# Row broadcasts for a state scan: one 128-partition transfer with a repeated source pattern in place of four 32-partition transfers

## The chip, the cores and the metric

The kernel runs on one core of one Trainium2 chip, as one program in one launch. The metric is device time in microseconds (us) of one execution. Three executions before the change took 7948.8, 7950.06 and 7962.73 us; the median is 7950.06 us.

## The reference

The input `x` is 4 x 512 x 64 x 64 in float32, that is 4 batches of 512 channels and 4096 positions. Two layers follow each other, each with a residual: `x = x + L0(groupnorm(x))`, then `x = x + L1(groupnorm(x))`. L0 is a state-space layer; L1 is a linear attention with 8 heads. The change lies in L0, whose core is this:

```python
xn = layer_norm(xf, norm_g, norm_b)                 # 512 channels, cut into 4 chunks of 128
xz = einsum('bld,ed->ble', chunk, in_proj_w); xi, z = split(xz, 2)      # 256 inner channels
xc = silu(causal_conv4(xi) + conv_b)
dbc = einsum('bld,ed->ble', xc, x_proj_w)
dt, Bs, Cs = dbc[..., :8], dbc[..., 8:24], dbc[..., 24:]
dt = softplus(einsum('blr,er->ble', dt, dt_proj_w) + dt_proj_b)
def step(h, inp):                                    # scan over 4096 positions
    dt_t, B_t, C_t, x_t = inp
    h = exp(dt_t[:, :, None] * A) * h + (dt_t * x_t)[:, :, None] * B_t[:, None, :]
    return h, einsum('bds,bs->bd', h, C_t)           # 16 states for each of 256 channels
y = (ys + xc * D_param) * silu(z)
ym = einsum('bld,od->blo', y, out_proj_w) + skip_scale * chunk
```

The row `B_t` of a state is the same for all channels, and so is the row `C_t`. On the chip each such row has to stand on every partition that holds a channel of that state.

## The kernel before

**Tiling.** The work is cut into steps `(b, t, c)`: 4 batches, 8 tiles of 512 positions (`T`), 4 chunks of 128 channels, so 128 steps. A step has 16 slots (`SLOTS`), 2,048 in all. The 256 inner channels of a step are two halves `e` of 128. Within a half the 16 states are taken in `NQ` = 4 groups `q` of `KS` = 4 states. One tile holds 4 states x 32 channels (`BLK` = 32) on its 128 partitions: partitions 0 to 31 are the first state of the group, 32 to 63 the second, and so on. The four blocks of 32 channels, index `j`, lie side by side in the free dimension. A pair of slots (`jj` = 0, 1) handles one group `q` of one half.

**What a pair of slots does.**
- `b_row(g)` (line 692) brings the four B rows of a group to the 128 partitions of a tile `b_all`, 128 x 512 float32. There are three such buffers. It is called in the first slot of a pair, for the group three pairs on.
- `c_tail(g)` (line 697) does the same with the last quarter (128 positions) of the four C rows, into `c_sb`, 128 x 128 float32, two buffers. It is called in the second slot of a pair, for the next pair.
- Both call `for_states(dst, rows_, q)` (line 685), the function that is changed. `rows_` is a tile in DRAM, 16 rows of 512 (or of 128) positions, stored once per step at lines 659 and 660.
- `drive` (line 717, GpSimd) multiplies `d_all` by `b_all` into `bx`; it runs two slots ahead. `decay` (line 708, ScalarE) makes `dA` = exp(A dt); the scan at line 739 (VectorE) makes `h` from both.
- The product of `h` with the C row is cut in two. VectorE does 384 of the 512 positions (line 759), with a C row that TensorE brought into PSUM (`c_row`). GpSimd does the last 128 (line 751), with `c_sb`. TensorE then sums the states into `y`.

**Other transfers of the loop.** `spread` (line 633, transfers at line 639) is called twice in a step. It fills `d_all`, 128 partitions x 16 KB, from two DRAM tiles, with eight transfers of 256 KB, each to 32 partitions. Loads and stores of whole 1 MB tiles (`xn`, `xs`, `x`, `xa`, `xb`) and stores of results go by the same queue.

**What sets the order.** The order of instructions on each engine is written out by hand: `slot` calls the functions above, and `after` the work of neighbouring steps. All these transfers are issued by SyncE (SP) in program order. SP waits at a transfer for the buffer that it overwrites, and for the semaphore that it signals: there are eight of them, used in turn, and each transfer waits until the one eight before it has landed. Only the adding load `xr` is issued by GpSimd, and weight loads ahead of the loop by ScalarE.

Of the kernel before, what the change touches and what calls it, by code (L numbers as in the profile page):

```python
# [24 lines left out]
def kernel(  # L25
# [24 lines left out]
    nc = tc.nc  # L50
# [8 lines left out]
    BLK = 32  # L59
    KS = P // BLK  # L60
# [623 lines left out]

    def for_states(dst, rows_, q):

        for k in range(KS):
            nc.sync.dma_start(  # L688
                dst[k * BLK : (k + 1) * BLK, :], rows_[q * KS + k, :].partition_broadcast(BLK)
            )  # L690

    def b_row(g):
        n, e, q, _ = place(g)
        b_all[g // JJ] = wk.tile([P, T], F32, tag="b_all", name=f"b_all_{g}", bufs=3)
        for_states(b_all[g // JJ], fs[n]["b_rows"], q)

    def c_tail(g):
        n, e, q, _ = place(g)
        c_sb[g // JJ] = wk.tile([P, T - CUT], F32, tag="c_sb", name=f"c_sb_{g}", bufs=2)
        for_states(c_sb[g // JJ], fs[n]["c_rows"], q)  # L700
# [539 lines left out]
```

## Time and profile before

| What | Value |
|---|---|
| median of three executions | 7950.06 us |
| the profiled execution's own time | 7963.09 us |
| its span on the core | 7961.4 us |
| mean granted TensorE clock | 0.897 |
| busy VectorE (DVE), GpSimd (POOL) | 6977.7 us (88%), 6880.5 us (86%) |
| busy TensorE (PE), ScalarE (ACT) | 6453.6 us (81%), 5507.6 us (69%) |
| transfers to `b_all` | 4,096 of 64.0 KB |
| transfers to `c_sb` | 4,096 of 16.0 KB |
| transfers to `d_all` | 2,048 of 256.0 KB |

The profile is of one execution. A busy time counts the time in which an engine runs an instruction; the issuing of transfers by SP is not in it and is shown as `SPq`. DMA packets are the pieces that the 16 DMA engines of the core move one by one: a row of a transfer is one packet, and each engine that takes part in a transfer writes one more, of 4 bytes, to the semaphore at its end. "Share of 16 engines" is the summed time of packets over 16 times the length of the stretch; packets of one engine can overlap a little, so that it can pass 100%. The first 100 us are preparation and the first step's inputs, and the last 480 us are the rest of the attention of the last batch; the 2,048 slots lie between.

### The profile page before, as it was taken

To read this page: it belongs to the slowest core of one execution; us is meant where nothing else is said; L and a number is where in the kernel's file an instruction comes from. 1 tells how busy PE (TensorE), PEld (TensorE's weight loads), DVE (VectorE), ACT (ScalarE), POOL (GpSimd) and SP (SyncE) were. 2 spreads that over 40 slices of the span, in tenths; PEclk is the share of its full clock that TensorE was granted. 3 is DMA by queue.
4 is the path that set the end of the run, shared out by engine and by line. 5 is a ranking of instruction groups with operands and counts; after the bars stand their busy time and mean duration, and the time that the engine had idled before them with its cause. 6 is when DMAs were issued, how large, how long until landed. Compare 5 with 4: busy or idle time off the path is not lost.

```text
span 7961.4 us, 90563 instructions
## 1 busy us (share of the span) xinstructions
PE 6453.6 (81%) x24835; PEld 2120.0 (27%) x24880; DVE 6977.7 (88%) x5766; ACT 5507.6 (69%) x8321; POOL 6880.5 (86%) x4597
## 2 busy tenths in 40 slices
PE   5676777677789888888788888898688888888599
PEld 1121212112223222322222223332122332322144
DVE  5999999999999999989999999998999999988600
ACT  4667777777777777767777777677777777777421
POOL 4999999999999899989999899898999999889600
PEclk7888888888899999998899999899899999999799
DMA  5666666666666666777766666677666666676402
GB/s 154 167 168 166 151 155 159 160 155 167 169 179 162 151 163 159 174 189 175 174 155 171 171 157 161 155 185 189 156 167 163 161 161 159 145 194 180 112 32 90
DMA packets 829184, 1265.87 MB, mean 159 GB/s; under 512 B 183912, under 2 KB 317560, under 8 KB 816384
## 3 DMA queue, kind: packets, MB, share of 16 engines
q1 hardware_dynamic: 804736, 1222.32, 61.1%
q0 software_dynamic: 16896, 33.56, 2.4%
q10 hardware_dynamic: 7040, 4.20, 0.2%
q8 instruction: 195, 3.19, 0.2%
q14 instruction: 317, 2.60, 0.1%
HBM read 1052.78 MB, written 206.57 MB: 158 GB/s over the span
## 4 chain that ended last, share of the span: by engine, by line
DVE 33%; PE 21%; ACT 15%; DMA 12%; issue 8%; SPq 6%; POOL 6%; POOLq 0%; ACTq 0%; DVEq 0%
DVE h L739 22%; DVE h L759 9%; DMA d_all<-d_rows 7%; ACT dA L713 5%; PE pq L124 5%; POOL bx L721 4%; PE pc L124 4%; SPq L688 3%; PE y L124 3%; PE pr L124 3%; SPq L639 2%; DMA c_sb<-c_rows 2%; ACT xz L1048 2%; PE po L124 2%; ACT L1048 1%
## 5 line engine op out<-in xcount | busy, mean ns | idle before, releaser
L721 POOL TENSOR_TENSOR bx<-d_all,b_all 128x1024 f32<-128x1024 f32 x2048 | 4824.7, 2367 | 213.3 <-DVE h L739 195.1
L739 DVE TENSOR_TENSOR_SCAN h<-dA,st,bx 128x512 f32<-128x512 f32 x3584 | 4358.9, 1264 | 358.7 <-ACT dA L713 159.0
L713 ACT ACTIVATE dA<-d_all,a_t 128x512 f32<-128x512 f32 x4096 | 2752.9, 687 | 1568.5 <-DVE h L739 1521.8
L759 DVE TENSOR_TENSOR h<-h,c_all 128x1536 f32<-128x1536 f32 x1024 | 1767.5, 1726 | 0.1
L751 POOL TENSOR_TENSOR h<-h,c_sb 128x512 f32<-128x512 f32 x1024 | 1300.2, 1270 | 190.2 <-DMA c_sb<-c_rows 95.2
L124 PE MATMUL y<-h,fold 128*32 128x512 f32 x8192 | 1271.2, 696 | 71.6 <-POOL h L751 67.4
L124 PE MATMUL c_all<-parts,sel 128*128 128x384 bf16 x1024 | 369.9, 361 | 1123.3 <-DVE h L759 1121.7
L124 PE MATMUL pc<-xn,w_cv 128*128 128x512 f32 x2048 | 1045.7, 645 | 122.8 <-DVE xn L414 62.1
L124 PE MATMUL pq<-w_qk,xa 128*128 128x512 f32 x2048 | 965.5, 604 | 7.9 <-issue 5.3
L739 DVE TENSOR_TENSOR_SCAN h<-dA,bx 128x512 f32<-128x512 f32 x512 | 591.2, 1203 | 90.0 <-ACT dA L713 65.1
L124 PEld LDWEIGHTS <-sel 128*128 128x128 bf16 x1280 | 127.1, 99 | 1762.2 <-DVE h L759 1562.5
L124 PEld LDWEIGHTS pc<-xn,w_cv 128*128 128x128 f32 x2048 | 389.5, 201 | 747.1 <-issue 424.7
L124 PEld LDWEIGHTS pq<-w_qk,xa 128*128 128x128 f32 x2048 | 398.6, 196 | 439.6 <-issue 422.4
L124 PE MATMUL pr<-xb,m 128*128 128x512 f32 x1024 | 485.3, 612 | 7.5 <-DMA xb<-x 3.6
L124 PE MATMUL pp<-xn,w_pr 128*128 128x512 f32 x1024 | 477.7, 597 | 4.8 <-DVE xn L414 4.8
L124 PEld LDWEIGHTS y<-h,fold 128*32 128x32 f32 x8192 | 170.6, 114 | 644.0 <-issue 344.9
L124 PE MATMUL y<-xz,dg 32*32 32x512 f32 x2048 | 337.3, 734 | 0.0
L781 POOL TENSOR_TENSOR xz<-xz 128x512 f32<-128x512 f32 x256 | 325.7, 1272 | 9.2 <-ACT xz L778 9.2
L832 ACT ACTIVATE kq<-pq 128x512 f32<-128x512 f32 x256 | 150.5, 588 | 259.9 <-PE pq L124 259.2
L124 PE MATMUL pd<-xz,w_xp 128*128 128x512 f32 x512 | 323.4, 764 | 7.8 <-ACT xz L1048 7.8
L628 POOL TENSOR_TENSOR dt<-dt,xz 128x1024 f32<-128x1024 f32 x128 | 302.3, 2361 | 24.7 <-ACT dt L620 24.6
L124 PE MATMUL pz<-xn,w_z 128*128 128x512 f32 x512 | 275.4, 631 | 11.7 <-ACT xz L608 8.2
(179 smaller groups left out, 6034.1 us busy)
## 6 DMA issues: line engine op xcount, KB each, us to landing
d_all<-d_rows SPq DMA_DIRECT2D x2048, 256.0 KB, 6.7
b_all<-b_rows SPq DMA_DIRECT2D x4096, 64.0 KB, 2.2
d_rows<-dt SPq DMA_DIRECT2D x256, 512.0 KB, 3.6
c_sb<-c_rows SPq DMA_DIRECT2D x4096, 16.0 KB, 1.8
xs<-in_x_dram SPq DMA_DIRECT2D x32, 1024.0 KB, 6.3
xn<-in_x_dram SPq DMA_DIRECT2D x32, 1024.0 KB, 6.2
xr<-in_x_dram POOLq DMA_DIRECT2D x32, 1024.0 KB, 10.7
x<-xr SPq DMA_DIRECT2D x32, 1024.0 KB, 4.2
```

The source lines that it names most:

```text
L124: nc.tensor.matmul(out_, lhsT, rhs, **how)
L628: nc.gpsimd.tensor_tensor(f["both"][:, 1], f["both"][:, 0], f["xz"][:, 0], ALU.mult)
L639: nc.sync.dma_start(d[k * BLK : (k + 1) * BLK, v], src)
L688: nc.sync.dma_start(dst[k * BLK : (k + 1) * BLK, :], rows_[q * KS + k, :].partition_broadcast(BLK))
L713: nc.scalar.activation(dAs[k], fs[n]["d_all", e][:, 0, j, :], AF.Exp, scale=a_t[:, e, j, q : q + 1])
L721: nc.gpsimd.tensor_tensor(bxs[g], fs[n]["d_all", e][:, 1, jj * 2 : jj * 2 + 2, :], bc(b_all[g // JJ], 2), ALU.mult)
L739: nc.vector.tensor_tensor_scan(h[:, j, :], dAs.pop(2 * g + i), bxs[g][:, i, :], 0.0 if t == 0 else st[:, c, e, q, j : j + 1], ALU.mult, AL ...
L751: nc.gpsimd.tensor_tensor(h[:, :, CUT:], h[:, :, CUT:], bc(c_sb.pop(g // JJ), NJ), ALU.mult)
L759: nc.vector.tensor_tensor(own, own, bc(c_all.pop(g // JJ), NJ), ALU.mult)
L781: nc.gpsimd.tensor_tensor(f["xz"][:, 1, e, :], f["xz"][:, 1, e, :], f["xz"][:, 0, e, :], ALU.mult)
L832: nc.scalar.activation(qk[i], pq, AF.Relu)
L1048: nc.scalar.activation(fs[n]["xz"], fs[n]["xz"], AF.Silu)
```

## The change

`for_states` issues one transfer for all 128 partitions. Its source is the four rows of the group with a middle dimension of step 0 that repeats each row 32 times: 4 x 32 x 512 (or 128) elements. Its destination is the whole tile, 128 partitions x 512 (or 128). Bytes and rows are the same as those of the four transfers together: 128 rows of 2 KB, or of 512 bytes. Nothing else in the kernel changes.

```diff
     def for_states(dst, rows_, q):
 
-        for k in range(KS):
-            nc.sync.dma_start(
-                dst[k * BLK : (k + 1) * BLK, :], rows_[q * KS + k, :].partition_broadcast(BLK)
-            )
+        src = rows_[q * KS : (q + 1) * KS, :].unsqueeze(1).to_broadcast([KS, BLK, dst.shape[-1]])
+        nc.sync.dma_start(dst, src)
```

In the built program SP then has 1,024 transfers to `b_all` and 1,024 to `c_sb` in place of 4,096 each, in the same places of its order.

## The prediction

> **What bounds the kernel now.** I first read busy time by stage, since start and end have other limits than the loop.
>
> ```profile
> core 0: us, PE busy (x) PEld busy (x) DVE busy (x) ACT busy (x) POOL busy (x), PEclk, DMA share, GB/s
> 0.00:100.00 100.00, 43.65 (x103) 20.42 (x104) 39.28 (x92) 23.14 (x31) 2.89 (x13) 0.81 0.44 139
> 100.00:7480.00 7380.00, 5976.39 (x23219) 1902.78 (x23246) 6900.82 (x5591) 5376.73 (x8118) 6863.62 (x4573) 0.90 0.67 166
> 7480.00:7961.00 481.00, 433.59 (x1518) 196.81 (x1530) 37.56 (x83) 107.73 (x173) 13.96 (x13) 0.94 0.18 62
> ```
>
> In the loop, 7380 us for 128 steps or 57.66 us a step, VectorE is busy 93.5% and GpSimd 93.0%. These two bound it. The DMA engines have work 67% of the time: no bound, but no small reserve either. Next, who waits for the tiles that change, from the waits on GpSimd:
>
> ```profile
> POOL bx L721 <- DVE h L739: 195.1, 290, 6.6
> POOL h L751 <- DMA c_sb<-c_rows: 95.2, 63, 6.6
> ...
> POOL bx L721 <- DMA d_all<-d_rows: 16.4, 1, 16.4
> ```
>
> So late transfers cost GpSimd little: 95.2 us for `c_sb` and 16.4 us for `d_all`; the answer for `b_all` adds 12.9 us of waits on ScalarE. A faster broadcast has some 124 us to win, 1.6%, unless it frees something that these waits don't show. Then the DMA queues and, for the loop alone, their load:
>
> ```profile
> q10 hardware_dynamic: 7040, 4.20, 0.2%
> ```
>
> ```profile
> q1 hardware_dynamic: 790226, 1184.28, 64.4%
> q0 software_dynamic: 16368, 32.51, 2.5%
> q8 instruction: 182, 2.98, 0.2%
> q14 instruction: 311, 2.55, 0.1%
> ```
>
> The second fence is the loop's: 67.2% of 57.66 us is 38.7 us of packet time a step on each of the 16 engines.
>
> **What the change removes.** Of 8,192 issues on SP, 6,144 go. Line 688 has a median of 419 ns each in the line's answer, so a tile's four cost 1.68 us. The new pattern has three dimensions on the source. The nearest row for a form of issue that isn't this one is `a_t` at line 295, with 586 to 747 ns and a median of 595 ns; one new issue should cost 0.42 to 0.75 us, and I take 0.595. SP saves 4.0 us per pair of slots less 1.2 (two tiles), some 2.2 us of 3.4. This lies off the path: SP is ahead of GpSimd wherever its waits are for buffers (`SPq L688 <- POOL st`, 263.3 us) or for earlier landings (`SPq L688 <- DMA d_all`, 1555.2 us), and what reaches the engines of its lateness is within the 124 us. No instruction moves on the other engines, and no wait is added ahead of others on SP.
>
> **What it adds: fewer engines per transfer.** The number of engines that share a transfer is to be read from completion packets. This is a stretch in the preparation in which one weight load of 8 rows of 512 bytes (`w_dt`, 8 partitions) is moved:
>
> ```profile
> DMA packets 16, 0.00 MB, mean 10 GB/s; under 512 B 8, under 2 KB 16, under 8 KB 16
> ...
> q10 hardware_dynamic: 16, 0.00, 4.3%
> ```
>
> Eight rows and eight completions: 8 engines. A stretch of 2.4 us with four `c_sb` transfers alone has 128 rows, 64 completions (16 a transfer) and 10.0% of the 16 engines. From the two shares, 4.3% of 6.4 us and 10.0% of 38.4 us, a 512-byte row takes 26 ns and a completion 9. The whole ScalarE queue agrees: the shapes of its 27 loads make 6,680 rows, and the 7,040 packets leave 360 completions. That is 21 x 16 + 2 x 8 (`w_dt`) + 4 x 2 (`b_qk`, two partitions); sixteen for each would be 432. So an outermost count under 16 sets the number of engines, where both sides have the same count. The new transfer has 128 on the destination and 4 on the source, and no transfer of this trace has unequal counts. The bounds are 4 engines and 16. I take 4: an even cut of the outermost dimension has to fall on both sides, and four rows can't be dealt out to more than four. The Trainium skill, "DMA: Bandwidth & Descriptors", section "Why a DMA increments its semaphore by 16 and not by 1", says just this: the engines used are the largest number up to 16 that divides both outermost counts, and its "Rules for kernel authors" warn of a small outermost dimension. By the rule it is 4, and with the trace's rows alone it stays between 4 and 16.
>
> With 4 engines, each carries 32 rows of every B tile and 32 of every C tail; the other twelve carry none. Price of a 2 KB row, from three stretches:
>
> ```profile
> q1 hardware_dynamic: 783, 1.57, 103.8%
> ```
>
> ```profile
> q1 hardware_dynamic: 288, 0.30, 33.2%
> ...
> b_all<-b_rows SPq DMA_DIRECT2D x4, 64.0 KB, 2.0
> c_sb<-c_rows SPq DMA_DIRECT2D x4, 16.0 KB, 1.7
> ```
>
> ```profile
> q1 hardware_dynamic: 278, 0.49, 107.4%
> ...
> d_all<-d_rows SPq DMA_DIRECT2D x4, 256.0 KB, 6.6
> ```
>
> The first is 4 us of one 1 MB load to 128 partitions: 103.8% of 64 us over 783 packets is 85 ns. The second is 3 us with one B tile and parts of two C tails, 64 rows: 33.2% of 48 us is 15.9 us; less 96 completions at 9 ns and 64 C rows at 26 ns, 13.4 us is left for 128 B rows, 104 ns. The third is 2.5 us of `spread`, whose transfers go to 32 partitions: 107.4% of 40 us, less 35 completions and 6 small rows, over 237 rows is 179 ns. The same row of bytes thus costs 85 ns where all partitions are written and twice that where sixteen engines write 32. With 4 engines each would walk 32 partitions of its own. The bounds are 85 and 179 ns; I take 104, the same tile's own price.
>
> Load of one of the four engines in a step: today's 38.7 us less its part of B (64 rows, 6.7 us), C (64 rows, 1.7 us) and completions (64 at 9 ns, 0.6 us) leaves 29.7. Then 256 B rows at 104 ns are 26.6 us, 256 C rows at 26 ns 6.7, 16 completions 0.1. Sum 63.1 us, where the loop now takes 57.66. The four engines become the bound. At 85 ns it is 58.3 us, at 179 ns 82.3 (36.5 + 256 x the price).
>
> They can't be busy without a gap: eight transfers at most are under way, a B tile is asked for about four slots (14 us) before its use, and `spread` puts 64 rows on each engine at once. I allow 5%, a little less than the 6.5 and 7% that VectorE and GpSimd, which bind today, lose in the loop. That makes 66.3 us a step: 128 x 66.3 + 100 + 481 = 9067 us. Two effects stand against each other and are not in it: rows that meet `spread` cost more, and `spread`'s own rows meet fewer others. The profiled execution has 2 us around its span, and the median is 13 us (0.2%) under it; I round to 9000 us. What covered the old arrangement was even loading, 38.7 of 57.7 us on every engine; now twelve engines fall to 30 us and four pass the step. What is late next are `b_all` and `c_sb` at GpSimd, and `d_all`, which queues behind them on the same four engines; VectorE waits for both.
>
> **The rivals.**
> - *Sixteen engines.* The pattern is cut finer on the source. Then each engine has 8 rows a tile, completions fall to a quarter, and the DMA waits above mostly go: 7963 - 124 = 7839 us at best, 7960 if nothing of it was on the path. For it: no row shows unequal counts. Against it: `w_dt` and `b_qk`. The Trainium skill, "SBUF — State Buffer", section "Door 1: The DMA port swizzle", speaks for the change here: 32 partitions reach half of the ports, 128 all. The trace agrees, 393 GB/s in the first stretch against 195 in the third; an estimate by that would make a B tile 0.7 us instead of 1.3, still within the 124 us. This rival decides if a B tile shows 16 completions.
> - *Four engines, which keep up.* At 85 ns the load is 58.3 us and some rows of `spread` get cheaper. The time lies between 8000 and 8300 us: 8043 by the sum, more by gaps. For it: the first stretch. Against it: B rows cost 104 today.
> - *Four engines that get in each other's way.* If two of the four write side by side as slowly as sixteen do in `spread`, 179 ns make 82.3 us a step and 581 + 128 x 82.3 = 11,115 us; halfway, at 141 ns, 72.6 us and 9874. It decides from about 137 ns (9700 us) on. For it: the third stretch. Against it: only four engines write here, to all partitions.
> - The change does what it says: the built program has one transfer per tile, so that no rival lies there.
>
> **How the numbers follow.** Sixteen engines 0.12; four that keep up (to 8300 us) 0.18; the forecast (8300 to 9700 us) 0.45; in each other's way 0.25. A measurement of this kernel can tell about 0.2%, 16 us, from no change. Faster by more: most of the first case, 0.10, and 0.01 of the second. Within: 0.04. Slower: 0.85. The range goes from 7980 us, which leaves out the first case and a little of the second, to 10,500 us, which leaves out some 0.06 of the last.
>
> **What would show it.** Right: four completion packets per transfer, so that packets under 512 bytes fall from 183,912 to about 61,000 (about 85,600 with sixteen); B tiles landing after 5 us or more in place of 2.2; GpSimd waiting hundreds of us for `b_all`, `c_sb` and `d_all`; busy shares of VectorE and GpSimd in the loop well under 93%; a DMA share that doesn't rise although transfers bind. Wrong: landings near 2 us, sixteen completions, or a loop at 57 us a step with GpSimd waiting less than today.

## The result and the profile after

The changed kernel took 8320.6 us (median of five, 8312.25 to 8334.17), against 7948.8 us before: a ratio of 1.0471, 95% interval 1.0453 to 1.0488. It became slower, as forecast, and by the mechanism that was forecast, but by 372 us where 1050 were forecast. Its profiled execution took 8320.6 us with a span of 8318.9 us.

First the number of engines, from the packet totals of the pages, before and after:

```profile
DMA packets 829184, 1265.87 MB, mean 159 GB/s; under 512 B 183912, under 2 KB 317560, under 8 KB 816384
```

```profile
DMA packets 706232, 1264.78 MB, mean 152 GB/s; under 512 B 61032, under 2 KB 194680, under 8 KB 693504
```

Packets under 512 bytes fell from 183,912 to 61,032. The 8,192 old transfers with 16 completions each made 131,072. With those gone and 8,192 new ones, the count is met: each of the 2,048 new transfers ends with exactly four. Four engines carry each of them. Then the waits, GpSimd's and SP's longest:

```profile
POOL h L749 <- DMA c_sb<-c_rows: 516.2, 208, 8.5
POOL bx L719 <- DVE h L737: 134.4, 167, 6.6
```

```profile
SPq L688 <- POOL st L748: 1860.7, 598, 8.6
SPq L688 <- DMA d_all<-d_rows: 569.0, 822, 1.9
SPq L639 <- DMA b_all<-b_rows: 535.3, 201, 6.7
```

(Lines stand two lower after the change: 749 was 751, 719 was 721, 737 was 739.) GpSimd's wait for `c_sb` rose from 95.2 to 516.2 us, while its wait for VectorE fell. SP has time to spare: its longest wait is now for GpSimd to give a buffer free. A new issue takes 513 ns (the median for `b_all`), inside the 420 to 750 ns that were allowed. VectorE's wait for `bx` rose from 78.0 to 444.4 us; before and after:

```profile
DVE h L739 <- POOL bx L721: 78.0, 70, 4.7
```

```profile
DVE h L737 <- POOL bx L719: 444.4, 199, 52.3
```

The loop, to be set beside the 7380 us of before:

```profile
100.00:7850.00 7750.00, 6083.11 (x23249) 1927.94 (x23277) 6932.93 (x5602) 5384.69 (x8127) 6863.97 (x4581) 0.88 0.63 158
```

GpSimd's busy time is the same, 6863.97 us where it was 6863.62, over a longer stretch: 88.6% busy, from 93.0%. The DMA share over all 16 engines is 0.63, lower than before. An average over 16 engines hides four that are full. A quiet stretch of 1.5 us, with broadcast rows alone, shows them:

```profile
DMA  2222214112222222221221222222222112222222
...
DMA packets 74, 0.15 MB, mean 101 GB/s; under 512 B 0, under 2 KB 0, under 8 KB 74
...
q1 hardware_dynamic: 74, 0.15, 26.3%
```

A digit of 2 means a busy share of 0.2 to 0.3, and four of 16 are 0.25. All 74 packets are 2 KB rows; 26.3% of 16 x 1.5 us over 74 is 85 ns a row. Four engines move 101 GB/s together, where the one load to 128 partitions before moved 393 with sixteen.

To compare kernels I take the loop from the first start of a `bx` product to the end of the last: 57.57 us a step before, 60.25 after. From the packet records of the trace one can also count how many packets are in flight at each moment. After, fewer than four are in flight in 5.1% of the loop (25.7% before), so all four engines can be busy together for 94.9% of it at most. A moment with one to three packets in flight still keeps some of the four at work. Counted in parts, their mean busy share is at most 96.3%.

### The profile page after: what moved, and what is told of

The parts are those of the page before. It is cut to its first block, busy times and chain, and to the rows that moved or that the text cites. A ratio compares the mean times of both kernels' runs of the same rounds, so it can differ in the third digit from the quotient of the medians.

```text
span 8318.9 us, 81269 instructions
## 1 busy us (share of the span) xinstructions
PE 6556.4 (79%) x24835; PEld 2146.6 (26%) x24880; DVE 6995.3 (84%) x5766; ACT 5510.3 (66%) x8321; POOL 6870.9 (83%) x4597
## 2 busy tenths in 40 slices
DMA packets 706232, 1264.78 MB, mean 152 GB/s; under 512 B 61032, under 2 KB 194680, under 8 KB 693504
## 4 chain that ended last, share of the span: by engine, by line
DMA 29%; DVE 20%; PE 19%; POOL 15%; ACT 9%; issue 7%; SPq 1%; POOLq 0%; ACTq 0%; DVEq 0%
DMA c_sb<-c_rows 15%; DVE h L737 13%; DMA d_all<-d_rows 11%; POOL bx L719 10%; DVE h L757 6%; PE pq L124 4%; PE y L124 3%; POOL h L749 3%; PE pc L124 3%; ACT dA L711 3%; PE pr L124 2%; DMA b_all<-b_rows 1%; PE po L124 1%; ACT xz L1046 1%; PE pp L124 1%
## 5 line engine op out<-in xcount | busy, mean ns | idle before, releaser
L749 POOL TENSOR_TENSOR h<-h,c_sb 128x512 f32<-128x512 f32 x1024 | 1300.5, 1270 | 643.5 <-DMA c_sb<-c_rows 516.2
L124 PE MATMUL y<-h,fold 128*32 128x512 f32 x8192 | 1314.2, 718 | 410.5 <-POOL h L749 403.7
L124 PE MATMUL pc<-xn,w_cv 128*128 128x512 f32 x2048 | 1078.6, 662 | 104.7 <-DVE xn L414 61.3
```

The source lines that it names most:

```text
L124: nc.tensor.matmul(out_, lhsT, rhs, **how)
L749: nc.gpsimd.tensor_tensor(h[:, :, CUT:], h[:, :, CUT:], bc(c_sb.pop(g // JJ), NJ), ALU.mult)
```

## The experiments

All times are medians, and each ratio is to runs of the kernel before on the same chip. Theory A is that the loss comes from four engines carrying all broadcast rows; theory B, that it comes from the form of the transfer, which lands only with its last row and is issued more slowly.

**More engines, same number of transfers.** The rows are stored `COPIES` times in DRAM, so that the outermost count of the source is 4 x `COPIES`.

```diff
-        b_rows = f["b_rows"] = dram.tile([NST, T], ...)
+        b_rows = f["b_rows"] = dram.tile([NST, COPIES, T], ...)      # c_rows likewise
-            nc.sync.dma_start(b_rows, dtr[RANK : RANK + NST, :])
+            nc.sync.dma_start(b_rows, copied(dtr[RANK : RANK + NST, :]))
...
-        src = rows_[q * KS : (q + 1) * KS, :].unsqueeze(1).to_broadcast([KS, BLK, dst.shape[-1]])
+        src = rows_[q * KS : (q + 1) * KS].rearrange("k c t -> (k c) t")
+        src = src.unsqueeze(1).to_broadcast([KS * COPIES, BLK // COPIES, dst.shape[-1]])
         nc.sync.dma_start(dst, src)
```

Four copies, 16 engines:

> One transfer per tile as in the changed kernel, but the DRAM rows are stored four times over, so that the outermost count of the source is 16 in place of 4. Theory A (the loss comes from four engines carrying all broadcast rows): 16 completions per transfer, packets under 512 bytes near 86,000, GpSimd waits for c_sb under 100 us, time 7830 to 7960 us. Theory B (the loss comes from the form: one transfer that lands only with its last row, issued at 513 ns): 8200 us or more, waits for c_sb near 500 us.

It took 7913.64 us, ratio 0.9949 (0.9934 to 0.9964), 0.5% faster than before.

```profile
DMA packets 743096, 1280.61 MB, mean 162 GB/s; under 512 B 85608, under 2 KB 225400, under 8 KB 730368
```

```profile
POOL bx L725 <- DVE h L743: 227.5, 359, 6.6
...
POOL h L755 <- DMA c_sb<-c_rows: 0.8, 1, 0.8
```

Now the completions are 16 a transfer, and the wait for `c_sb` is 0.8 us. Number, form and issue (520 ns) of the transfers are those of the changed kernel; theory B falls. The run also reads 16 rows of DRAM per transfer where the changed kernel reads four. That is hardly what helps: with four rows, four engines moved 101 GB/s in the quiet stretch above, 25 each, and the sixteen of the 1 MB load 393, also 25 each. The wait of 95.2 us that this run took away was worth 42 us only: GpSimd's wait for VectorE rose from 195.1 to 227.5 us in its place.

Two copies, 8 engines:

> The same with rows stored twice: 8 engines. Theory A: packets under 512 bytes near 69,000; each of the 8 engines carries 128 B rows and 128 C rows a step, some 44 us of 58, so that little is late: 7860 to 8050 us. Theory B: 8200 us or more.

7910.39 us, ratio 0.9944 (0.9928 to 0.9961).

```profile
DMA packets 718520, 1270.06 MB, mean 161 GB/s; under 512 B 69224, under 2 KB 204920, under 8 KB 705792
```

Eight engines are as good as sixteen; it takes the last halving to hurt.

**One kind of tile at a time.** In both, the kernel before is changed for one size of `dst` alone, `== T` for the B rows or `< T` for the C tails:

```diff
     def for_states(dst, rows_, q):
+        if dst.shape[-1] == T:
+            src = rows_[q * KS : (q + 1) * KS, :].unsqueeze(1).to_broadcast([KS, BLK, dst.shape[-1]])
+            nc.sync.dma_start(dst, src)
+            return
```

> Only the B rows come in one transfer on four engines, the C tails in four transfers on sixteen. Theory A: the four engines lose 256 - 64 C rows a step, some 5 us of load of some 58; most of the loss stays: 8080 to 8280 us. Theory B with the C tail's own transfer as the slow part: 7900 to 8000 us.

B rows alone took 8072.95 us, ratio 1.0148 (1.0133 to 1.0163), just under the range. GpSimd waits 224.6 us, and it waits for C tails, which have sixteen engines here:

```profile
POOL h L755 <- DMA c_sb<-c_rows: 224.6, 110, 8.7
```

So a tile can be late although its own transfer is as before. What fits is that four of its sixteen engines are behind with B rows, and it lands with the last; the trace doesn't name the engine of a packet.

> Only the C tails come in one transfer on four engines, the B rows in four transfers on sixteen. Theory A: the four engines carry some 44 us a step, nothing binds, and SP issues 3,072 transfers fewer: 7880 to 7990 us. Theory B with the C tail's own transfer as the slow part: 8150 to 8320 us, GpSimd waiting 400 us or more for c_sb.

C tails alone took 7912.48 us, ratio 0.9948 (0.9933 to 0.9962), with 14.3 us of waits for `c_sb`:

```profile
POOL h L755 <- DMA c_sb<-c_rows: 14.3, 11, 4.3
```

The parts don't add: against before, B alone costs 117 us, C alone gains 43, and both together cost 372. A sum of two prices can't give that, a bound that is passed can.

**Short of time, or late in bursts?** A third `c_sb` buffer, and each C tail called one pair earlier:

```diff
-        c_sb[g // JJ] = wk.tile([P, T - CUT], F32, tag="c_sb", name=f"c_sb_{g}", bufs=2)
+        c_sb[g // JJ] = wk.tile([P, T - CUT], F32, tag="c_sb", name=f"c_sb_{g}", bufs=3)
...
-        elif g + 1 < last:
-            c_tail(g + 1)
+        elif g + 1 + JJ < last:
+            c_tail(g + 1 + JJ)
```

> The changed kernel with three c_sb buffers in place of two and each C tail called one pair of slots earlier (small tiles of once-a-batch work give up their second buffers to make the room). Theory A1 (the four engines are short of time as a whole): the loop stays near 60 us a step, 8230 to 8330 us. Theory A2 (they have the time, but spread puts its rows ahead of a C tail that is needed soon): the waits for c_sb go from 516 us to under 150, 8000 to 8150 us.

8253.13 us, ratio 1.0373 (1.0357 to 1.0388): theory A1. The wait didn't go, it changed its name:

```profile
POOL bx L719 <- DMA b_all<-b_rows: 398.5, 143, 9.8
POOL bx L719 <- DVE h L737: 134.2, 162, 6.6
```

With a longer lead for C, GpSimd waits for `b_all`. The step is 59.74 us, with fewer than four packets in flight in 3.4% of the loop, from 5.1%. What was gained is a part of the gaps.

> The kernel before with the same third c_sb buffer and earlier C tail. Its waits for c_sb were 95 us: both theories expect them nearly gone and 7870 to 7950 us; it is the control for the run with the changed kernel.

The control took 7929.77 us, ratio 0.9968 (0.9957 to 0.9979), inside its range. The product with `c_sb` waited 0.4 us for its transfers, from 95.2; another 40.1 us are put down to `c_sb` at the `bx` product, which doesn't read that tile. The time fell by 28 us.

> One transfer per tile on sixteen engines (rows stored four times) and the third c_sb buffer with the earlier C tail. What is left of waits for c_sb should go: 7860 to 7915 us, against 7914 without the third buffer.

7918.8 us, ratio 0.9951 (0.9935 to 0.9968), just over the range: nothing on top of sixteen engines alone, where no wait for `c_sb` was left. Four kernels thus beat both the one before and the changed one, by 0.5% against before: 16 engines with and without the third buffer, 8 engines, and C tails alone on 4. Between them these runs show no difference.

**The price of a row.** Two transfers per tile, each for 64 partitions with an outermost source count of 2:

```diff
-        for k in range(KS):
-            nc.sync.dma_start(
-                dst[k * BLK : (k + 1) * BLK, :], rows_[q * KS + k, :].partition_broadcast(BLK)
-            )
+        for k in range(0, KS, 2):
+            src = rows_[q * KS + k : q * KS + k + 2, :].unsqueeze(1).to_broadcast([2, BLK, dst.shape[-1]])
+            nc.sync.dma_start(dst[k * BLK : (k + 2) * BLK, :], src)
```

> Two transfers per tile, each for 64 partitions with an outermost source count of 2, so that two engines carry all broadcast rows: 512 B rows and 512 C rows a step each, with some 30 us of other rows. Theory A1 with 85 ns a B row: 30 + 43.5 + 13.8 = 87 us a step, 11,500 to 12,000 us. With the 104 ns of the prediction: 97 us a step, 12,700 to 13,200 us. Theory A2 has no other number here; were the engines not the bound, it would stay under 9000 us.

11,296.72 us in two executions, ratio 1.4199 (1.4167 to 1.4231): under the range for 85 ns a row, and far from that for 104. A stretch of 40 us shows two engines at work, 0.12 of 16, between the bursts of `spread`:

```profile
DMA  1111111111111115992111111111111499999966
GB/s 31 27 33 25 35 29 41 51 49 51 49 52 45 49 51 205 408 409 88 46 57 49 49 53 49 51 51 43 45 49 57 76 311 190 209 158 164 215 145 162
```

The step is 83.45 us, and fewer than two packets are in flight in 0.2% of the loop only. So two engines are all but full: at most 83.3 us of load a step = other rows + 512 B rows + 512 C rows. In the changed kernel all four engines can be busy for 60.25 x 0.949 = 57.2 us a step, and their mean load is at most 60.25 x 0.963 = 58.0 us = other rows + 256 B + 256 C. If the other rows cost the same in both kernels, the difference of 25.3 to 26.1 us for 256 pairs is 99 to 102 ns a pair. With a C row at 27 ns (the median of the packet records) a B row would be 72 to 75 ns.

The packet records speak against that "if". I take the stretches of the loop, 0.7 us and longer, in which only 2 KB rows are in flight, at least one and at most two for each engine that carries the broadcasts, and leave out 0.1 us at both ends. That is 990 us of the changed kernel, with 46,406 rows on four engines, and 2625 us of this one, with 61,945 rows on two. Counted over time, not from their own records, a row takes its engine 85 ns in both (990.5 x 4 / 46,406 and 2624.8 x 2 / 61,945). At 85 ns, B and C rows make 28.7 us of the changed kernel's step and 57.3 us of this one's, and other rows are left with 28.5 to 29.3 us there and 26.0 here. The bursts, with 14 packets or more in flight, are also shorter here, 23.8 us a step against 26.6. So the 72 to 75 ns are a difference between two kernels, not the price of a row. Why the other rows cost less here is open.

Two other runs test the 85 ns. B alone should be 28.5 to 29.3 us, 256 x 85 ns and 64 x 27 ns, in sum 52.0 to 52.8 us of load; the trace has 52.2 us with all four busy and 53.8 of mean load at most. The run with the third buffer moves the same rows as the changed kernel, 57.2 to 58.0 us; it has 57.7 and 58.6.

## Why the prediction was right and wrong

**Right:** four engines, from the completion packets of loads in the trace; which engine would wait (GpSimd, then VectorE on `bx`); that SP's saved issues would not show; and, nearly, the 5% for gaps: the four were not all busy in 5.1% of the loop, and idle for at least 3.7% of it in the mean.

**Wrong: the size of one term, the price of a B row.** The sum against what the runs showed, per step:

| Term | Prediction | Runs |
|---|---|---|
| other rows on each of the four | 29.7 us | 28.5 to 29.3 us, what the load leaves |
| 256 B rows | 26.6 us (104 ns) | 21.8 us (85 ns) |
| 256 C rows | 6.7 us | 6.9 us |
| load | 63.1 us | 57.2 to 58.0 us |
| with gaps | 66.3 us | 60.25 us |
| 128 steps | 8486 us | 7712 us |

The 774 us between the last two numbers are the miss. The step that failed is the price of a B row: 104 ns in the sum, 85 ns where the rows follow each other on one engine. That is 4.8 of the 5.1 to 5.9 us by which the load was too high; the rest is spread over the other rows and can't be told apart. The nearest row was the wrong one: of the three stretches I took the one with the same tile. There each engine has two rows of a transfer and then waits for the next, and some rows' recorded times seem to hold waiting too. The 128 B rows of that stretch have a mean of 105 ns, but a median of 84. Over the whole loop before, rows that start with at most ten packets in flight have 117 and 84. After the change 32 rows follow each other on one engine, as in the load to 128 partitions, which gave 85 ns. The likeness that mattered was the length of the run, not the tile.

One figure of the SP sum was wrong, without effect: eight issues at 419 ns are 3.4 us a pair of slots, not 4.0, and less 1.2 they leave the 2.2 that the text goes on with.

Of the rivals, *four engines, which keep up* came true, but for its upper end: it gave 8043 us by the sum and 8300 us with gaps. Its load, 58.3 us, was within 2% of the measured 57.2 to 58.0. The rival's 8043 us had no gaps in it, though the forecast's sum had; with 5% it would have been 61.4 us a step or some 8440 us, 1.4% over the measured time. *In each other's way* was wrong: the four engines didn't slow each other, at 85 ns a row with four at work as with two. *Sixteen engines* was wrong for the change itself; the runs that made it so gave 7914 and 7919 us, within the 7839 to 7960 us of its price, and a third of the 124 us of waits was won.

**Points of the list.** Completions as forecast (about 61,000); GpSimd's busy share down as forecast; the DMA share didn't rise. GpSimd's waits of hundreds of us were for `c_sb` alone, not for `b_all` and `d_all` (23.6 us). The profile gives no landing time for transfers that end with four completions, so the forecast of 5 us or more was not seen.

## What to carry to other kernels

Before joining transfers, count on how many DMA engines the joined one will run: completion packets tell it, and where source and destination have different outermost counts the runs here followed the smaller one. A DMA share averaged over sixteen engines says nothing of four that are full; work out the load of the busiest engine per step and set it beside the step. For its price take a stretch in which rows follow each other as they will, not the same tile in another rhythm.

## What the runs showed of the hardware

- An outermost count of 2, 4, 8 and 16 on the source, with 64 or 128 partitions on the destination, ran on 2, 4, 8 and 16 engines: 61,032 small packets for 4,096 transfers on 2 or 2,048 on 4, 69,224 for 2,048 on 8, 85,608 on 16.
- Load close to the step already costs: B rows alone fill the four engines to between 52.2 and 53.8 us, where the loop with sixteen engines takes 57.19 us, and still 1.1 us a step is lost.
- A 2 KB row took its engine 85 ns where such rows followed each other, with four engines at work and with two, and 85 ns in the load on sixteen to 128 partitions.
- An issue on SP with the three-dimensional source took 513 ns, against 419 ns for the one before.
